# Pacing the next batch's preparation in a two-layer graph attention kernel

## The chip, the cores and the metric

The kernel runs on one core of one Trainium2 chip. The metric is the device time of one execution in microseconds (us); lower is better.

## The reference

The input `x` is 8 batches of 2048 nodes with 256 features, and `adj` is a 2048 x 2048 adjacency matrix. Two layers run one after the other, each on `relu(layernorm(x))` and with a residual. The first is an attention over chunks of keys with a normalised output. The second, which the change concerns, is a graph attention with four heads of 64 features:

```python
q = (h @ W).reshape(B, N, H, D)
e_src = einsum('bnhd,d->bnh', q, a[:D])
e_dst = einsum('bnhd,d->bnh', q, a[D:])
e = e_src[:, :, None, :] + e_dst[:, None, :, :]
e = where(e >= 0, e, 0.2 * e)
e = where(adj > 0, e, NEG_INF)
h_prime = einsum('bijh,bjhd->bihd', softmax(e, axis=2), q)
x = x + elu(h_prime.reshape(B, N, H * D))
```

For a batch this needs first `h`, the scores `e_src` and `e_dst`, and `q`; then, for all pairs of nodes, the weights and the weighed sums.

## The kernel before

The second layer runs from about 2785 us of the profile to its end, batch after batch. A batch is cut into 4 *passes* (a pair of heads `hp` and a half of the 2048 query nodes `half`), and a pass into 16 *rounds*, one for each tile `jt` of 128 keys. So a batch has 64 rounds, and the layer 512. In this text P0 to P3 are the four passes of a batch, and "P2, round 10" is the round with `jt` 10 of the third.

In a round (the loop at L903):

- VectorE (DVE) makes the weights `e` of the round *after the next*, one instruction of 128x1024 for each of the two heads (`clipped`, L809). They are built as a maximum of two terms and a clip by the mask `limit`. The terms that depend on the query (`near`) are made once for a pass by ScalarE (ACT) from the rows `es`, which a DMA spreads over the partitions (`nears`, L798; `sources`, L784).
- TensorE (PE) multiplies `e` by the rows `qn` and sums in `acc` (`weigh_rows`, L820).
- For the softmax's denominator, rounds are taken in pairs: ACT scales the `e` of the even round (tile `t`, L924), GpSimd (POOL) adds that of the odd one (L928), and two rounds later PE sums the result over the keys (`add_up_rows`, L832, in `den`). The last pair of a pass is not added by POOL; PE sums both.
- At the end of a pass ACT copies `acc` and `den` out of PSUM (`cT`, L933; `dT`, L942), and the work to finish the pass is queued (`ending`): PE turns `dT` and `cT` round (`flip`, L156), DVE inverts and multiplies (L855, L866), ACT and POOL make the ELU and the residual (L875 to L881), and SP stores.

What is done beside the rounds stands in a list, `aside`, of generators. At the end of each round `advance` takes one step of each:

```python
def advance(all_of=True):
    moved = all_of and tick()
    for steps_of in list(aside):
        got = next(steps_of, aside)
        ...
        if got is None:
            ...
            break
    return moved
```

A step that yields None has given PE a piece of work, and ends the call; one that yields True has given work to the other engines alone, and False none, and the next generator gets its turn. Each round therefore has at most one such piece of PE work. `ending` is put in front of the list. In round 13 of a pass `advance` is not called. All pieces use one PSUM area (`aux`), so each waits until the one before has been read.

The *preparation* of a batch (`preparation`) is one of these generators. Its steps are, in order:

1. `roots` on POOL (L132 to L135) makes 1/deviation and the offset for the 16 tiles of rows; the second is a power of 128x16 elements (L133).
2. For each of the four blocks of 512 rows: ACT makes `h` (L144), PE turns it round in two pieces (L156) and ACT copies it to `hT` (L164); then a third piece of PE work (L606) makes the scores, and ACT copies them to `er` (L613). SP loads the rows of the next block at the begin of a block (L110).
3. DVE takes the extremes (`ends`, L618, L619); SP sends `er` and `ends` to DRAM and the spread extremes back (`gm`, L622 to L626). After three further steps DVE reads `gm` (L635, L636), with small operations on ACT and POOL (`spans`, `least`).
4. PE turns `er` round (one piece), DVE makes `far` and `logs` (L649, L651), then POOL `quot` and ACT three exponentials and `for_sums`.
5. Eight *sides*: PE makes a quarter of a block's `q` (L153 in `sides`, 16 matmuls as the kernel writes them, 32 in the trace), and DVE writes it to `qn` with the share of its key (L676).

That is 21 pieces of PE work. The preparation of batch b + 1 is put in the list in the first round of batch b. It is needed when the rows `es` for the next batch's first pass are fetched, in P3, round 8, where the kernel drains the list until it is done (L916). Each engine works in the order in which its instructions were issued.

Of the kernel before, what the change touches and what calls it, by code (L numbers as in the profile page):

```python
# [51 lines left out]
def layers(  # L52
# [40 lines left out]
    def pair(dtype=F32):  # L93
        n = QB if dtype == F32 else 2 * QB
        return psum.tile([P, 2, n], dtype, tag="big", name="big", bufs=3)

    def banks(name):
        return [psum.tile([P, QB], F32, tag=f"both{k}", name=name) for k in range(2)]
# [6 lines left out]
    def heads_tile(name, tag, bufs=2):  # L105
        return big.tile([P, 2, QB], F32, tag=tag, name=name, bufs=bufs)
# [86 lines left out]
    aside = []  # L193

    quiet = []
    here = [-3]
# [15 lines left out]
# [5 lines that stand above are left out]
            if got is aside:  # L217
                aside.remove(steps_of)
            moved = moved or got is not False
            if got is None:  # L220
                if here[0] < 0:
                    aside.append(aside.pop(aside.index(steps_of)))
                break
        return moved

    def drain(until=lambda: False):
        while not until() and advance():
            pass
# [157 lines left out]
    for name, w in (("q", Wq), ("k", Wk), ("v", Wv), ("o", Wo)):  # L386
# [4 lines left out]
        if name == "o":  # L391

            got = big.tile([P, FC, F], F32, tag="c", name="w_halves")
# [81 lines left out]
    def divide(sums):  # L475

        s = big.tile([P, QB], F32, tag="s", name="s", bufs=1)
        nc.scalar.copy(s, sums)  # L478
        got = small.tile([P, 16], F32, tag="sum", name="sum")
        nc.sync.dma_start(got, s[0:P:32, :].rearrange("h (j i) -> h j i", i=16))  # L480
        return got
# [221 lines left out]
    steps = [(b, qb, c) for b in range(B) for qb in range(NQB) for c in range(NCH)]  # L703
# [27 lines left out]
    for n in range(-2, len(steps)):  # L731
        here[0] = n
        if n >= 0:
            b, qb, c = steps[n]
# [21 lines left out]
        if inside:  # L756
            sums = pair()[:, 0, :]
            add_up(weights[n + 1][1], sums)
            got = divide(sums)
# [19 lines left out]
    def sources(held, hp, half):  # L779

        es = []
        for hh in range(2):
            e = big.tile([P, HALF], F32, tag="add", name="es")
            nc.sync.dma_start(  # L784
                e,
                held[2 * hp + hh, 2 * half : 2 * half + 2, :, :]
                .rearrange("b c p -> (b c p)")
                .partition_broadcast(P),
            )
            es.append(e)  # L790
        return es
# [24 lines left out]
    def weigh_rows(jt, hp, es, qn, acc):  # L816

        for blk in range(2):
            for q in range(4):
                nc.tensor.matmul(  # L820
                    acc[blk][32 * q : 32 * q + 32, :],
                    qn[jt // NT][:, jt % NT, hp * P + 32 * q : hp * P + 32 * q + 32],
                    es[q // 2][:, blk, :],
                    start=(jt == 0),
                    stop=(jt == NKT - 1),
                )

    def add_up_rows(m, hp, parts, for_sums, den):

        for k, ts in enumerate(parts):  # L830
            for q in range(4):
                nc.tensor.matmul(  # L832
                    den[32 * q : 32 * q + 32, :],
                    for_sums[:, m, 2 * hp + q // 2, :],
                    ts[q // 2][:, q % 2, :],
                    start=(m == 0 and k == 0),
                    stop=(m == NKT // 2 - 1 and k + 1 == len(parts)),
                )

    def mine(to, blk, hp):  # L840

        return to[blk * QB : (blk + 1) * QB, hp * P : (hp + 1) * P].rearrange("(t p) f -> p t f", p=P)

    def ending(k, cT, dT):
# [15 lines left out]
        for blk in range(2):  # L860
# [21 lines left out]
            yield True  # L882
            nc.sync.dma_start(mine(out[b], 2 * half + blk, hp), xh)

    LAG = 2
    places = [pair() for _ in range(3)]
    rest.append(places[2])
# [5 lines left out]
    def begun(k, jt):  # L893

        b, hp, half = passes[k]
        if jt == 0:
            near[:] = nears(following.pop(k), hp, shared[b][2])
        return clipped(jt, hp, half, near, shared[b][3])
# [2 lines left out]
    ready = [begun(*rounds[0]), begun(*rounds[1])]  # L901
    due, ts, acc, den = [], None, None, None
    for s, (k, jt) in enumerate(rounds):  # L903
        here[0] = len(steps) + s // 4
        b, hp, half = passes[k]
        qn, held, off_s, far, quot, for_sums = shared[b]
        if s + 2 < len(rounds):
            ready.append(begun(*rounds[s + 2]))
        now = ready.pop(0)
        if jt == 0:  # L910
            acc = banks("acc1")
            if hp == half == 0 and b + 1 < B:
                aside.append(preparation(b + 1))
        if jt == (2 if k % 4 < 3 else 8) and k + 1 < len(passes):
            b1, hp1, half1 = passes[k + 1]
            drain(lambda: b1 in shared)  # L916
            following[k + 1] = sources(shared[b1][1], hp1, half1)
        weigh_rows(jt, hp, now, qn, acc)
        if jt % 2 == 0:
            ts = []  # L920
            for hh in range(2):
                t = heads_tile("t", "q", 4)
                h = 2 * hp + hh
                nc.scalar.activation(t, now[hh], AF.Copy, scale=quot[:, jt // 2, h : h + 1])  # L924
                ts.append(t)
        elif jt + 1 < NKT:
            for hh in range(2):
                nc.gpsimd.tensor_tensor(ts[hh], ts[hh], now[hh], ALU.add)  # L928
            due.append((s + LAG, jt // 2, [ts]))
        else:  # L930
            cT = big.tile([P, 2, QB], F32, tag="hT", name="cT", bufs=1)
            for blk in range(2):
                nc.scalar.copy(cT[:, blk, :], acc[blk])  # L933
            due.append((s, jt // 2, [ts, now]))
        while due and due[0][0] <= s:
            _, m, parts = due.pop(0)
            if m == 0:
                den = rest[0][:, 0, :]
            add_up_rows(m, hp, parts, for_sums, den)
        if jt == NKT - 1:  # L940
            dT = const.tile([P, QB], F32, tag="wk", name="dT")
            nc.scalar.copy(dT, den)  # L942
            aside.insert(0, ending(k, cT, dT))

        if jt != NKT - 3:
            advance()
# [252 lines left out]
@with_exitstack  # L1199
def adj_preln_kernel(  # L1200
    ctx: ExitStack,
    tc: tile.TileContext,
    x, adj, Wq, bq, Wk, bk, Wv, bv, Wo, bo, gamma, beta, W, a, out,
):
    nc = tc.nc
    B, N, F = x.shape
    const = ctx.enter_context(tc.tile_pool(name="const", bufs=1))
    dram = ctx.enter_context(tc.tile_pool(name="dram", bufs=1, space=bass.MemoryType.DRAM))
    ident = const.tile([P, P], F32, tag="ident", name="ident")
    make_identity(nc, ident)  # L1210
    x1 = [dram.tile([N, F], F32, tag=f"x1_{b}", name=f"x1_{b}") for b in range(B)]
    verdict = const.tile([1, 1], I32, tag="verdict", name="verdict")
    layers(
        tc, x, adj, Wq, bq, Wk, bk, Wv, bv, Wo, bo, gamma, beta, W, a, x1, out, ident, dram, verdict
    )
    with tc.If(nc.values_load(verdict, min_val=0, max_val=1) != 0):
        gat_layer(tc, x1, adj, W, a, out, ident)
# [35 lines left out]
```

## Time and profile before

| | |
|---|---|
| median of 3 runs | 4297.43 us (4297.36 to 4297.71) |
| profiled execution, its own time | 4298.93 us |
| its span in the profile | 4297.1 us |
| busy PE, POOL, DVE, ACT | 95%, 79%, 75%, 59% of the span |
| second layer: first weighing of rows | 2785.2 us |
| e of the second layer, DVE | 1024 instructions, mean 1275 ns |
| adds of the second layer, POOL | 448 instructions, mean 2388 ns |
| granted PE clock in the second layer | 1.00 from 2800 us to 4200 us |

The busy shares are means over two layers whose limits differ. For the second layer the traces are read pass by pass. A pass is taken here from the end of one copy of `dT` to the end of the next, since everything that a pass makes ends in it. Busy times count an instruction from its start to its end; where they overlap in an engine's pipeline, the price of one more is the distance from start to start, and that is what is used.

### The profile page before, as it was taken

To read this page: it belongs to the slowest core of one execution; us is meant where nothing else is said; L and a number is where in the kernel's file an instruction comes from. 1 tells how busy PE (TensorE), PEld (TensorE's weight loads), DVE (VectorE), ACT (ScalarE), POOL (GpSimd) and SP (SyncE) were. 2 spreads that over 40 slices of the span, in tenths; PEclk is the share of its full clock that TensorE was granted. 3 is DMA by queue.
4 is the path that set the end of the run, shared out by engine and by line. 5 is a ranking of instruction groups with operands and counts; after the bars stand their busy time and mean duration, and the time that the engine had idled before them with its cause. 6 is when DMAs were issued, how large, how long until landed. Compare 5 with 4: busy or idle time off the path is not lost. (4 is left out here: it accounts for less than half of the span.)

```text
span 4297.1 us, 86491 instructions
## 1 busy us (share of the span) xinstructions
PE 4103.1 (95%) x34742; PEld 1452.8 (34%) x34742; DVE 3221.3 (75%) x3974; ACT 2527.1 (59%) x3194; POOL 3409.1 (79%) x1795
## 2 busy tenths in 40 slices
PE   7889999999999999999999999989999999999998
PEld 3333333333333333333333333323333233333322
DVE  4676766666667666666666567689898898988997
ACT  4555555555655565555555567565666656566665
POOL 2467787887788788788788778878887888887897
PEclk9999999999999999999999999999999999999999
DMA  3221121122112111112211121211221212122121
GB/s 100 81 90 49 47 59 57 47 55 60 47 54 62 49 52 54 57 47 54 61 49 52 59 61 46 86 57 52 60 70 33 75 52 67 53 59 70 33 62 34
DMA packets 280267, 248.16 MB, mean 58 GB/s; under 512 B 95792, under 2 KB 230704, under 8 KB 279856
## 3 DMA queue, kind: packets, MB, share of 16 engines
q1 hardware_dynamic: 275248, 225.76, 18.7%
q0 software_dynamic: 4608, 16.78, 1.0%
q8 instruction: 275, 4.51, 0.5%
q14 instruction: 136, 1.11, 0.1%
HBM read 204.15 MB, written 36.18 MB: 56 GB/s over the span
## 5 line engine op out<-in xcount | busy, mean ns | idle before, releaser
L448 DVE SCALAR_TENSOR_TENSOR E<-big,limit 128x1024 f32<-128x1024 f32 x1024 | 1182.7, 1217 | 653.3 <-PE big L440 647.1
L725 POOL TENSOR_TENSOR add<-E 128x1024 f32<-128x1024 f32 x512 | 1203.5, 2372 | 569.8 <-PE both L460 474.2
L454 ACT ACTIVATE E<-E 128x1024 f32<-128x1024 f32 x1024 | 1055.0, 1057 | 540.3 <-DVE E L448 521.9
L809 DVE SCALAR_TENSOR_TENSOR e<-big,far,limit 128x1024 f32<-128x1024 f32 x1024 | 1239.6, 1275 | 39.5 <-POOL t L928 18.3
L928 POOL TENSOR_TENSOR t<-t,e 128x1024 f32<-128x1024 f32 x448 | 1055.2, 2388 | 226.7 <-ACT t L924 225.6
L820 PE MATMUL acc<-e,qn 128*32 128x512 f32 x8192 | 1035.6, 596 | 5.6 <-DVE e L809 5.5
L440 PE MATMUL big<-qT,kT 64*128 64x512 f32 x4096 | 966.8, 609 | 43.0 <-DVE E L448 35.6
L460 PE MATMUL both<-E,v 128*32 128x512 f32 x8192 | 991.9, 596 | 0.5 <-DVE c L498 0.2
L924 ACT ACTIVATE t<-e,quot 128x1024 f32<-128x1024 f32 x512 | 561.4, 1142 | 267.9 <-PE big L832 165.0
L440 PEld LDWEIGHTS big<-qT,kT 64*128 64x128 f32 x4096 | 366.3, 187 | 589.9 <-issue 384.1
L500 POOL TENSOR_TENSOR acc<-acc,c 128x1024 f32<-128x1024 f32 x224 | 530.3, 2368 | 1.4 <-DVE c L498 1.4
L460 PEld LDWEIGHTS both<-E,v 128*32 128x32 f32 x8192 | 274.9, 110 | 601.8 <-issue 345.7
L820 PEld LDWEIGHTS acc<-e,qn 128*32 128x32 f32 x8192 | 274.5, 110 | 504.8 <-issue 462.0
L832 PE MATMUL big<-t,for_sums 128*32 128x512 f32 x2048 | 359.3, 596 | 62.3 <-POOL t L928 51.1
L498 DVE TENSOR_TENSOR c<-both,r 128x512 f32<-128x512 f32 x448 | 308.8, 690 | 44.3 <-PE both L460 17.3
L471 PE MATMUL big<-add,ones 128*32 128x512 f32 x2048 | 282.7, 610 | 12.2 <-DVE E L448 1.8
L478 ACT COPY s<-big 128x512 f32<-128x512 f32 x256 | 150.1, 586 | 81.2 <-PE big L471 81.1
L832 PEld LDWEIGHTS big<-t,for_sums 128*32 128x32 f32 x2048 | 76.2, 109 | 282.2 <-POOL t L928 172.2
L164 ACT COPY hT<-big 128x512 f32<-128x512 f32 x128 | 74.2, 580 | 135.2 <-PE big L156 135.2
L144 ACT ACTIVATE h<-x,off,rstd 128x256 f32<-128x256 f32 x256 | 139.1, 592 | 4.7 <-POOL off L135 4.7
L337 ACT ACTIVATE qT<-big,bq 128x512 f32<-128x512 f32 x64 | 44.0, 687 | 153.9 <-PE big L153 153.9
L318 ACT COPY v<-big 128x512 f32<-128x512 f32 x64 | 37.4, 584 | 157.4 <-PE big L153 120.1
(116 smaller groups left out, 3122.3 us busy)
## 6 DMA issues: line engine op xcount, KB each, us to landing
r<-inv SPq DMA_DIRECT2D x1024, 64.0 KB
x<-in_x_dram SPq DMA_DIRECT2D x96, 512.0 KB
es<-er SPq DMA_DIRECT2D x64, 512.0 KB
adj_in<-in_adj_dram SPq DMA_DIRECT2D x32, 512.0 KB
x<-o POOLq DMA_DIRECT2D x32, 512.0 KB, 3.3
x<-x SPq DMA_DIRECT2D x32, 512.0 KB
xh<-x SPq DMA_DIRECT2D x64, 256.0 KB
out_dram<-xh SPq DMA_DIRECT2D x64, 256.0 KB
```

Source lines behind the costliest of these rows:

```text
L440: nc.tensor.matmul(ps[:, hh, :], ks[kt // NT][own, hp, (kt % NT) * P : (kt % NT + 1) * P], qs[qb][own, hp, :], start=True, stop=True,)
L448: nc.vector.scalar_tensor_tensor(e, ps, -0.5, bcast(limit[:, qb, kt, :], 1, 2), ALU.max, ALU.min)
L454: nc.scalar.activation(e, e, AF.Exp, scale=0.25 * EDGE)
L460: nc.tensor.matmul(both[part][32 * h : 32 * h + 32, :], vs[kt // NT][:, kt % NT, mine], es[h // 2][:, h % 2, :], start=first, stop=not first,)
L498: nc.vector.tensor_tensor(to[:, part, :], both[part], r, ALU.mult)
L500: nc.gpsimd.tensor_tensor(acc, acc, to, ALU.add)
L725: nc.gpsimd.tensor_tensor(both, tiles[0][hp], tiles[1][hp], ALU.add)
L809: nc.vector.scalar_tensor_tensor(e, near[hh], far[:, jt, h : h + 1], limit[:, 2 * half : 2 * half + 2, jt, :], ALU.max, ALU.min,)
L820: nc.tensor.matmul(acc[blk][32 * q : 32 * q + 32, :], qn[jt // NT][:, jt % NT, hp * P + 32 * q : hp * P + 32 * q + 32], es[q // 2][:, blk, :],
L832: nc.tensor.matmul(den[32 * q : 32 * q + 32, :], for_sums[:, m, 2 * hp + q // 2, :], ts[q // 2][:, q % 2, :], start=(m == 0 and k == 0), s ...
L924: nc.scalar.activation(t, now[hh], AF.Copy, scale=quot[:, jt // 2, h : h + 1])
L928: nc.gpsimd.tensor_tensor(ts[hh], ts[hh], now[hh], ALU.add)
```

## The change

The generator of the preparation is wrapped in another, which lets a step pass only when its time has come. After the n-th piece of PE work it yields False until 2.5 n rounds have gone by since the preparation's first step, so that the 21 pieces are spread over some 52 of the batch's 64 rounds. Steps without PE work are let through. Where the kernel drains the list, the flag `hurry` lifts the limit.

```diff
+    at, hurry = [0], [False]
+
+    def paced(steps_of):
+
+        first, done = at[0], 0
+        for got in steps_of:
+            yield got
+            if got is None:
+                done += 1
+                while 2 * (at[0] - first) < 5 * done and not hurry[0]:
+                    yield False
+
...
-        here[0] = len(steps) + s // 4
+        here[0], at[0] = len(steps) + s // 4, s
...
-                aside.append(preparation(b + 1))
+                aside.append(paced(preparation(b + 1)))
         if jt == (2 if k % 4 < 3 else 8) and k + 1 < len(passes):
             b1, hp1, half1 = passes[k + 1]
+            hurry[0] = True
             drain(lambda: b1 in shared)
+            hurry[0] = False
             following[k + 1] = sources(shared[b1][1], hp1, half1)
```

No instruction is added or left out; their order on the engines is another. Seven batches are prepared in this way, in batches 0 to 6. The preparation of batch 0 itself, which falls in the first layer, is as before, and the last batch has none to make.

## Prediction

> **What bounds the kernel now.** I read the page first: no engine is at its end in the mean, so the second layer has to be read by pass. The busy times by stretch, one row for each pass of a usual batch (here batch 4; the fifth row is a pass of batch 7, which prepares nothing):
>
> ```profile
> core 0: us, PE busy (x) PEld busy (x) DVE busy (x) ACT busy (x) POOL busy (x), PEclk, DMA share, GB/s
> 3550.21:3597.51 47.30, 43.83 (x380) 13.62 (x374) 40.13 (x36) 32.77 (x46) 41.52 (x22) 1.00 0.24 77
> 3597.51:3642.89 45.38, 44.26 (x400) 14.25 (x404) 41.00 (x42) 31.42 (x44) 38.49 (x21) 1.00 0.20 52
> 3642.89:3694.49 51.60, 51.60 (x602) 20.25 (x598) 44.56 (x44) 26.81 (x34) 38.03 (x18) 1.00 0.07 22
> 3694.49:3737.11 42.62, 39.92 (x346) 12.26 (x340) 41.30 (x38) 25.95 (x31) 37.87 (x18) 1.00 0.31 97
> ...
> 4153.46:4196.13 42.67, 39.94 (x344) 12.41 (x340) 39.85 (x36) 25.94 (x31) 37.94 (x18) 1.00 0.16 51
> ```
>
> P0 to P3 take 47.30, 45.38, 51.60 and 42.62, together 186.9 us; four bare passes would take 170.7. So preparation costs 16.2 us a batch, and each pass has its own reason. Next the timelines. First POOL, at the begin of a bare pass, of P0 with its roots, and of P1:
>
> ```profile
> 4154.59 9.44 POOL L928 TENSOR_TENSOR t<-t,e 128x1024 f32<-128x1024 f32 x4 [4.58 <-ACT t L924]
> ...
> 3556.49 2.92 POOL L133 TENSOR_TENSOR rstd<-rstd,power 128x16 f32<-128x16 f32 x1
> ...
> 3600.95 9.45 POOL L928 TENSOR_TENSOR t<-t,e 128x1024 f32<-128x1024 f32 x4 [7.62 <-ACT t L924]
> ```
>
> A bare pass is POOL's: its first add starts 1.13 after the end of `dT`, 14 adds and 4 operations of the ending follow without a gap until 4192.67 (38.08), and 3.47 later the last sums are out and `dT` is copied: 42.67. P0 is the same plus the roots, 3.87 us on POOL (3556.15 to 3560.02), plus 0.7 at the end, where PE is late: 47.3. P1 is the same with POOL's start 3.44 after `dT`, not 1.13. ACT shows why:
>
> ```profile
> 3596.92 0.59 ACT L942 COPY dT<-big 128x512 f32<-128x512 f32 x1 [1.86 <-PE big L832]
> 3598.26 0.59 ACT L164 COPY hT<-big 128x512 f32<-128x512 f32 x1 [0.75 <-PE big L156]
> 3598.74 1.09 ACT L144 ACTIVATE h<-x,off,rstd 128x256 f32<-128x256 f32 x2
> 3599.73 4.26 ACT L924 ACTIVATE t<-e,quot 128x1024 f32<-128x1024 f32 x4
> ```
>
> A step of preparation in P0, round 15, stands between `dT` and the next pass's `t`, for which POOL waits. P2 is PE's: the timeline has no gap (here in the P2 of batch 3), and the chain of waits of batch 4's P2 holds nothing but PE (last line):
>
> ```profile
> 3472.78 1.90 PE L820 MATMUL acc<-e,qn 128*32 128x512 f32 x16
> 3474.49 1.91 PE L153 MATMUL big<-w,hT 128*32 128x256 f32 x32
> 3476.22 1.90 PE L820 MATMUL acc<-e,qn 128*32 128x512 f32 x16
> 3477.94 1.04 PE L832 MATMUL big<-t,for_sums 128*32 128x512 f32 x8
> 3478.79 1.91 PE L153 MATMUL big<-w,hT 128*32 128x256 f32 x32
> ...
> by line: PE acc L820 55.5%; PE big L153 26.8%; PE big L832 15.1%; PE big L156 3.4%
> ```
>
> From start to start, a round's products take 1.72, a side 1.73, a pair's sums 0.85. P2 is 16 x 1.72 + 9 x 0.85 + 3 flips x 0.72 (0.59, and 0.13 on the next product) = 37.4, and 8 sides are 13.8: 51.2 of the measured 51.6.
>
> Here a rule weighs against the reading. The Trainium skill ("Perfetto Trace Analysis", Identifying the Most-Contended Engine) says that matmul busy time is no good measure of headroom, and to take weight-load busy time. That is 20.25 of 51.60 in P2, 39%: PE would have room, moving sides out of P2 would bring nothing there, and the sum below would be -0.4 a batch. But my sum uses spacing, not durations, and it fills the pass; the row decides for PE.
>
> **The change part by part.** The order of the changed program's instructions, engine by engine, gives the places of the 21 pieces in a usual batch. Before: P0 rounds 6, 7, 8, 10, 11, 12, 15; P1 2, 3, 6, 7, 8, `er` in 14; sides in P2 3, 5 to 11. After: P0 6, 7, 8, 11, 12, 15; P1 3, 5, 6, 10, 11, 14; `er` in P2 7; sides in P2 10, 11, 12, 14, 15 and P3 2, 3, 5. So the change spreads, but not evenly: the DMA trip for `gm` and six steps without PE work hold the sides back to P2, round 10.
>
> *P0.* The roots stay in round 2 and POOL bounds as before. One piece less lies ahead of the end, so some of the 0.7 of PE's lateness goes: 46.9, **-0.4** (0 to -0.7).
>
> *P1.* Round 15 of P0 now holds the scores (L606, 0.44 on PE beside the 0.59 of `dT`), and ACT the copy of `er` (0.25) instead of a wait for a flip, `hT` and two `h`. POOL starts at about 1.3. `spans` and `least` move to P2. The piece in round 14 adds up to 0.44 at the end: 1.3 + 38.1 + 3.9 = 43.3, **-2.1** (-1.4 to -2.3, the whole delay). The turns in rounds 3 and 5 put ACT's `hT` behind PE; I reckon `t` for round 4 ready at 13.5 to 14.7 after `dT`, POOL's need at 13.3 to 15.7: just in time.
>
> *P2.* Until round 9 POOL bounds it: in a bare pass the sums of round 9 get their last add at 25.15 after `dT` (3719.64 in P3), now 0.45 later for `spans` and `least`, so they are done at 26.0. Then PE has six products (10.3), five sums (4.3), and the sides of 10, 11, 12, 14 (6.9); with `dT` 0.6: 48.1, **-3.5**. DVE has `ends`, `far`, `logs`, `top` and four `qn` more (1.2 + 0.5 + 4 x 0.6) than the 39.9 and 2.7 idle of a bare pass: 46.7, below it. The new order on SP puts `gm` behind a fetch of `es`, which waits for ACT's L798 of round 14 of the pass before, so it is long issued. From `ends` to `gm` took 8.2 (3625.06 to 3633.25), the cover is now 8 e x 1.19 + 0.6 = 10.1. If that cover went, DVE's slack of 1.4 is next; bounds 0 to +2.
>
> *P3.* Four sides fall after P2's `dT` (round 15 of P2 and 2, 3, 5). PE: 37.4 + 6.9 + 0.4 = 44.7 if it never waits. `qn` is a new wait on DVE: in order, the e of three rounds ahead and the ending's `z` stand behind it. Following PE piece by piece, the side of round 3 ends 14.0 after `dT`, `qn` 14.6, the next e 17.0, the second `z` 17.6, its ELU 19.7, when POOL wanted it at 17.8: POOL loses 1.9, 44.5. I take 44.7, **+2.1** (+0.4 if PE's slack of 5 takes the sides, +6.9 if each side is paid whole).
>
> A usual batch: -0.4 - 2.1 - 3.5 + 2.1 = **-3.9**, six times: -23.4.
>
> *Batch 0* (58.4, 51.7, 51.3, 42.7) carries the end of the first layer. In P0 a turn leaves rounds 7 to 9, where ACT waited 4.0 for a flip behind 64 matmuls of L153: -1 (0 to -3). P1 loses two sides at its end, where the last add is followed by 4.6, not 3.5, and `spans`, `least`, `quot` (0.6): -2. P2 keeps six sides, later; by the same walk 49.0: -2.3. P3 with two has room: +0.3. **-5** (-1 to -8).
>
> Sum -28.4 against the profiled span of 4297.1. That execution's own time, 4298.93, is 1.5 above the median; its 1.8 outside the span don't change. Predicted: 4297.4 - 28.4 = 4269.0.
>
> **The rivals.** About 0.2%, 8.6 us, is what a measurement of this kernel can tell from no change.
>
> *More (10%).* PE's idle time in P3 takes its four sides: P3 43.0, P2 47: -6.7 a batch, with batch 0 about -47, 4250. For it: PE idles 5 us in a bare pass. Against: those idle stretches are short and late, the sides early.
>
> *Nothing that can be told (14%).* P3 gives back P2's gain (48), or P1's `er` waits longer: near 0, about 4292 to 4300. For it: PE, DVE and POOL are within 10% of each other.
>
> *Slower (11%).* One mechanism: DVE waits for each late side and passes the wait on to POOL through e. Then every side in P2 from round 10 and in P3 is paid on top of POOL's pass: P2 42.7 + 0.9 + 6.9 + 0.7 = 51.2, P3 49.6, together 6.6 above now; less 2.5 in P0 and P1 that is +4.1 a batch, +28 in seven, 4326. It decides once P2 and P3 together exceed 96.7. For it: DVE has 2.7 of idle time a pass, and waits in order. Against: e is two rounds ahead and has five rounds of buffers.
>
> *The pacing has no effect* is excluded by the order above; that it is half used is in the sum.
>
> **The numbers.** The likeliest case (65%, 4255 to 4286) gives 4269. Faster 0.76: that case, "more", and a little of the next. Within 0.2%: 0.13. Slower: 0.11. The range 4250 to 4295 takes in the bounds, half of "more" and half of "nothing".
>
> **What would show it.** P2 near 48 and P3 near 44.7, with `qn` in both; PE without a gap from P2 round 9 to P3 round 5; POOL's first add of P1 1.3 after `dT`, and a wait of about 2 us before an `L880` in P3. It is wrong if P3 is above 48, or P2 stays above 50, or DVE waits for `gm`.

## The result and the profile after

The changed kernel takes 4296.57 us (median of 12 runs, 4293.9 to 4301.18), the kernel before 4297.38 in the runs beside it: a ratio of 0.9998, with a 95% interval of 0.9989 to 1.0006. No difference can be told. The prediction was 4269.0, faster, with a range that ended at 4295.0.

The work was moved as the change says, and each pass took part. The busy times by stretch of the changed kernel, P0 to P3 of batch 4, cut at the same marks as before (the end of each copy of `dT`):

```profile
core 0: us, PE busy (x) PEld busy (x) DVE busy (x) ACT busy (x) POOL busy (x), PEclk, DMA share, GB/s
3546.09:3593.55 47.46, 43.80 (x364) 13.34 (x358) 41.07 (x38) 31.52 (x43) 41.49 (x22) 1.00 0.28 90
3593.55:3637.93 44.38, 43.47 (x412) 14.65 (x416) 40.35 (x37) 32.16 (x45) 37.90 (x18) 1.00 0.17 50
3637.93:3686.60 48.67, 46.03 (x468) 21.20 (x460) 41.91 (x44) 27.36 (x36) 38.41 (x21) 1.00 0.11 26
3686.60:3733.87 47.27, 47.06 (x480) 17.68 (x482) 43.38 (x41) 25.71 (x31) 38.02 (x18) 1.00 0.26 67
```

| us | P0 | P1 | P2 | P3 | batch | its change |
|---|---|---|---|---|---|---|
| before (batch 4) | 47.30 | 45.38 | 51.60 | 42.62 | 186.90 | |
| predicted | 46.9 | 43.3 | 48.1 | 44.7 | 183.0 | -3.9 |
| after | 47.46 | 44.38 | 48.67 | 47.27 | 187.78 | +0.88 |

P2 gives 2.9 and P1 1.0; P3 takes 4.65. Six such batches make +5.3. Batch 0 gives about 3.1 (56.4, 51.1, 50.6, 43.0 in place of 58.4, 51.7, 51.3, 42.7), and 0.4 less is spent behind the last pass. So the second layer, from its first product to the end of the span, grew from 1512.0 to 1513.7. The rest of the difference between the two profiled spans lies in the first layer, whose instructions are the same: it ended at 2785.2 in the one and at 2781.6 in the other, and between 2779.0 and 2786.5 in the other kernels below that leave it alone. For that reason the passes of batch 4 are compared here, and the medians stand beside them. From batch to batch a pass mostly repeats within 0.05 us (P1 of the kernel before within 0.25, P2 of e2 within 0.35, P1 of e6 within 0.64).

**P3.** How its begin looks in the timeline, PE's rows first, then DVE's:

```profile
3684.78 1.20 PE L832 MATMUL big<-e,for_sums 128*32 128x512 f32 x6
3686.66 1.93 PE L153 MATMUL big<-w,hT 128*32 128x256 f32 x32 [0.69 <-ACT dT L956]
3688.41 1.90 PE L820 MATMUL acc<-e,qn 128*32 128x512 f32 x16
3690.24 0.66 PE L156 MATMUL big<-ident,dT 128*128 128x128 f32 x4
...
3688.73 0.69 DVE L676 TENSOR_TENSOR qn<-big,share 128x512 f32<-128x512 f32 x1 [3.93 <-ACT t L938]
3689.33 2.47 DVE L809 SCALAR_TENSOR_TENSOR e<-big,far,limit 128x1024 f32<-128x1024 f32 x2
3691.72 0.25 DVE L855 RECIPROCAL inverse<-big 128x16 f32<-128x16 f32 x1
...
3701.51 0.69 DVE L676 TENSOR_TENSOR qn<-big,share 128x512 f32<-128x512 f32 x1 [0.99 <-PE big L153]
...
3708.25 0.69 DVE L676 TENSOR_TENSOR qn<-big,share 128x512 f32<-128x512 f32 x1 [0.69 <-PE big L153]
3708.86 26.45 DVE L809 SCALAR_TENSOR_TENSOR e<-big,far,limit 128x1024 f32<-128x1024 f32 x22
```

The side of P2's round 15 is given out after the copy of `dT`. PE has done the last sums and stands for 0.69 until that copy ends (3686.60); then come the side, and only behind it the next round's product and the flip of `dT`. DVE idles 3.93 before the `qn` of that side. (The row names ACT's `t`; but the `qn` reads the side, which ended at 3688.59, 0.14 before the `qn` began.) DVE takes up the ending (`inverse`) 5.12 after the end of `dT`. In P3 before this was 1.77, for there the next round's product had run beside the copy. Two more waits for sides follow (0.99, 0.69), then 22 e without a gap. So the e of round 15 is complete at 41.41 after `dT`, not at 34.42. What hangs on it stands in ACT's rows:

```profile
3726.85 2.31 ACT L798 ACTIVATE big<-es,off_s 128x1024 f32<-128x1024 f32 x2 [3.52 <-DVE e L809]
3729.10 2.17 ACT L938 ACTIVATE t<-e,quot 128x1024 f32<-128x1024 f32 x2
3731.18 1.04 ACT L947 COPY cT<-acc 128x512 f32<-128x512 f32 x2
3733.28 0.59 ACT L956 COPY dT<-big 128x512 f32<-128x512 f32 x1 [1.06 <-PE big L832]
```

`near` for the next pass (L798) can be made only when the last e has read the old one; ACT waits 3.52 for it. The `t` of round 14 (L924 before, L938 here), itself long possible, stands behind `near` in ACT's order, and PE's last sums wait for that `t`. From the e of round 15 (called the last e from here on) to the end of `dT` it is 5.86. In P3 before there were 8.20, since the last sums waited for POOL's adds (the row of PE):

```profile
3696.27 0.26 DVE L855 RECIPROCAL inverse<-big 128x16 f32<-128x16 f32 x1 [0.33 <-PE big L156]
...
3727.75 2.31 ACT L798 ACTIVATE big<-es,off_s 128x1024 f32<-128x1024 f32 x2 [1.13 <-DVE e L809]
...
3733.70 1.48 PE L832 MATMUL big<-t,for_sums 128*32 128x512 f32 x10 [0.19 <-POOL t L928]
...
3736.52 0.59 ACT L942 COPY dT<-big 128x512 f32<-128x512 f32 x1 [2.39 <-PE big L832]
```

That is 2.3 of slack. In the changed kernel POOL's last add ends 5.36 before the end of the pass, in P3 before 3.46, so POOL no longer bounds it. The excess is DVE's: 3.35 from the late begin, 1.8 for three `qn` at 0.60, 1.7 for the two waits, less 2.3 of slack: 4.5 of the 4.65 measured.

**P1.** The piece of P0's round 15 meets the same wait, in the rows of PE, ACT and POOL:

```profile
3593.60 0.64 PE L606 MATMUL big<-hT,wa 128*32 128x128 f32 x16 [0.70 <-ACT dT L956]
...
3594.32 0.27 ACT L613 COPY er<-big 128x128 f32<-128x128 f32 x1 [0.77 <-PE big L606]
3594.48 4.27 ACT L938 ACTIVATE t<-e,quot 128x1024 f32<-128x1024 f32 x4
...
3595.70 9.40 POOL L942 TENSOR_TENSOR t<-t,e 128x1024 f32<-128x1024 f32 x4 [6.53 <-ACT t L938]
```

The scores' matmuls begin when `dT` has been copied, not beside it; ACT's copy of `er` waits for them and `t` for that copy. POOL starts 2.15 after `dT`: less than the 3.44 of before, more than the 1.3 foretold. Its last add ends at 40.21, and the pass 4.17 later, where the kernel before had 41.88 and 3.50.

### The profile page after: what moved, and what is told of

Read it like the earlier page. It is cut to its first block, busy times and chain, and to the rows that moved or that the text cites. A ratio compares the mean times of both kernels' runs of the same rounds, so it can differ in the third digit from the quotient of the medians.

```text
span 4295.3 us, 86471 instructions
## 1 busy us (share of the span) xinstructions
PE 4109.3 (96%) x34742; PEld 1498.4 (35%) x34742; DVE 3219.6 (75%) x3974; ACT 2525.9 (59%) x3194; POOL 3408.8 (79%) x1795
## 5 line engine op out<-in xcount | busy, mean ns | idle before, releaser
L938 ACT ACTIVATE t<-e,quot 128x1024 f32<-128x1024 f32 x512 | 560.2, 1141 | 204.4 <-PE big L832 96.3
L820 PEld LDWEIGHTS acc<-e,qn 128*32 128x32 f32 x8192 | 291.9, 110 | 499.4 <-issue 419.9
L153 PE MATMUL big<-w,hT 128*32 128x256 f32 x2048 | 141.7, 380 | 4.2 <-ACT dT L956 4.1
```

The lines of the kernel that those rows point to most:

```text
L820: nc.tensor.matmul(acc[blk][32 * q : 32 * q + 32, :], qn[jt // NT][:, jt % NT, hp * P + 32 * q : hp * P + 32 * q + 32], es[q // 2][:, blk, :],
```

## The experiments

Two theories stood at first. A: the piece in round 15 costs, by what it makes PE, DVE and ACT wait for. B: P3 has simply too much PE work with four sides; its PE row is busy for 47.06 of 47.27. The total times in the expectations are for a kernel before of some 4297; each ratio is to runs of the kernel before beside that experiment. All kernels below are named by their labels.

**e1_after_no15.** The changed kernel with round 15 closed to the preparation:

```diff
-        for got in steps_of:
-            yield got
+        while True:
+            while at[0] % NKT == NKT - 1 and not hurry[0]:
+                yield False
+            got = next(steps_of, paced)
+            if got is paced:
+                return
+            yield got
```

> The changed kernel, with no step of the preparation in round 15 of a pass (it waits for round 2 of the next). Still four sides fall in P3 (rounds 2, 3, 5, 6 instead of P2 15 and P3 2, 3, 5). Theory A (the piece of round 15 is what costs: PE's piece waits for the copy of dT, and what DVE or ACT does with it stands ahead of the next pass's work): P1 from 44.4 to 43.5, P3 from 47.3 to about 44.9, together -3.3 a batch, some 4274 us. Theory B (four sides in P3 are simply too much PE work, wherever they lie): P3 stays at 46.5 to 47.3, P1 43.5, some 4289 us.

Measured: 4281.4 us, ratio 0.9960 (0.9946 to 0.9973).

```profile
3590.60:3633.99 43.39, 42.92 (x408) 14.91 (x404) 40.33 (x37) 31.96 (x46) 37.95 (x18) 1.00 0.18 56
3633.99:3682.64 48.65, 46.66 (x480) 22.15 (x474) 43.72 (x46) 27.36 (x36) 38.40 (x21) 1.00 0.09 26
3682.64:3728.12 45.48, 45.48 (x474) 16.63 (x468) 41.75 (x40) 25.49 (x31) 37.97 (x18) 1.00 0.27 74
```

P1 is 43.39 (from 44.38) and P3 45.48 (from 47.27), with the same four sides in it. DVE takes up the ending 1.78 after `dT` again, and its fourth `qn` and a longer sum of waits take back part of the 3.35. Theory A holds, 0.6 short in P3; what is left, 2.9 above a bare pass, is the price of four sides in P3. P3's PE row is full here too, which is why A needed more than this run: the PE row was full in both and P3 differed by 1.8.

**e2_before_no15.** The same closing of round 15 in the kernel before, without any pacing.

> The kernel before, without pacing, with no step of the preparation in round 15 alone. The turning of er moves from P1 round 14 to P2 round 2, and the sides to P2 6 to 12 and 14. Theory A: P1 from 45.4 to 43.3, P2 no better than 51.6 to 52.5, so about -1.5 a batch, 4287 us. Theory B says nothing of P1; if P1 stays at 45.4 the place of round 15 is not what costs there, and the time is that of before or slightly above.

Measured: 4285.7 us, ratio 0.9970 (0.9959 to 0.9980).

```profile
3589.23:3631.88 42.65, 42.55 (x396) 15.08 (x390) 40.77 (x40) 30.98 (x45) 38.24 (x20) 1.00 0.21 55
3631.88:3683.95 52.07, 52.07 (x600) 23.51 (x598) 45.65 (x47) 27.19 (x34) 38.23 (x19) 1.00 0.08 22
```

P1 falls by 2.7 to a bare pass's time, more than the 2.1 expected: POOL starts 1.12 after `dT` in place of 3.44, and its `spans` and `least` stand behind its last add, no longer between the adds (0.4 more). P2 rises by 0.5. This one condition brings more than the whole change.

**e3_sides_spread.** As e2, and the eight sides alone paced:

```diff
+        first, done = 0, 0
...
+            if got is None:
+                done += 1
+                if done == 13:
+                    first = at[0]
+                while done > 13 and 2 * (at[0] - first) < 5 * (done - 13) and not hurry[0]:
+                    yield False
```

> The kernel before with no step in round 15 and only the eight sides paced, one per two and a half rounds (the first 13 pieces as soon as they can): sides in P2 6, 7, 8, 11, 14 and P3 2, 3, 5. Theory A: P1 43.3, P2 47, P3 44.5, P0 47.3: 182 a batch, -4.7, some 4265 us. Theory B: P3 with three sides 45.5, P2 47.5: 183.6 a batch, some 4275 us.

Measured: 4265.81 us, ratio 0.9924 (0.9911 to 0.9938), the fastest of all.

```profile
3532.93:3580.24 47.31, 44.47 (x388) 13.99 (x386) 41.55 (x38) 32.76 (x46) 41.56 (x22) 1.00 0.29 91
3580.24:3622.91 42.67, 42.55 (x396) 15.06 (x390) 40.80 (x40) 30.97 (x45) 38.26 (x20) 1.00 0.21 55
3622.91:3669.80 46.89, 46.89 (x504) 19.72 (x502) 43.29 (x44) 27.08 (x35) 38.22 (x19) 1.00 0.08 24
3669.80:3714.21 44.41, 44.27 (x444) 16.47 (x438) 41.23 (x39) 25.49 (x31) 37.96 (x18) 1.00 0.27 73
```

As theory A had it, within 0.7 of each pass. Against e2 only the sides moved: P2 loses three of them and 5.2 us, which is 3 x 1.73; P3 gains three and 1.8. So there is a gain in spreading the sides, 3.4 a batch, once round 15 is kept free. It depends on where they begin. The spreading of the change itself, with round 15 free (e1), brings nothing in a usual batch against e2 (185.0 and 184.7); what it brings, it brings in batch 0 (201.6 and 207.7). In e1 the sides begin in P2, round 10, in e3 in round 6, and P2 is 1.8 shorter in e3 though it holds one side more. (The pieces ahead of the sides lie elsewhere in the two as well.)

**e4_late_qn.** The changed kernel, each `qn` given out at the begin of the next call of `advance`, behind one more round of e:

```diff
-                nc.vector.tensor_tensor(
...
+                def keep(q=q, ps=ps, n=n, two=two, blk=blk):
+                    nc.vector.tensor_tensor(
...
+                quiet.append(keep())
                 yield
...
```

> The changed kernel; DVE's qn is issued one round after its side (behind the e of that round) and nothing else moves: the side of P2 round 15 stays where it is and still waits for the copy of dT, and PE has the same work. Theory A (DVE waiting in order for the side, ahead of e): P3 from 47.3 to 44.9 to 45.5, P1 stays at 44.4, about -2 a batch, 4283 us. Theory B: P3 stays at 47.3, 4297 us.

Measured: 4318.26 us, ratio 1.0043 (1.0029 to 1.0057); P2 49.75, P3 47.33. A miss for theory A as it was put. The timeline at the end of P2 shows a wait that took the place of the one removed:

```profile
3705.44 0.69 DVE L678 TENSOR_TENSOR qn<-big,share 128x512 f32<-128x512 f32 x1 [5.25 <-ACT dT L962]
...
3706.19 1.93 PE L153 MATMUL big<-w,hT 128*32 128x256 f32 x32 [1.43 <-DVE qn L678]
```

The `qn` of round 14, now given out after the copy of `dT`, waits for that copy, and the next side waits for the `qn`, as it fills the same PSUM area. DVE's ending begins 5.05 after `dT`, as in the changed kernel, and the last e is complete at 41.47. So this run didn't take the wait away, and says nothing of its price. Why P2 rose by 1.1 was not followed up. The edit also reaches the first batch's preparation in the first layer, which ended at 2793.8; its second layer took 1523.5.

**e5_e_first.** The changed kernel, with DVE's e for round 2 of the next pass ahead of the step of round 15:

```diff
-        if s + 2 < len(rounds):
+        if s + 2 < len(rounds) and (jt or not s):
             ready.append(begun(*rounds[s + 2]))
...
+        if jt == NKT - 1 and s + 3 < len(rounds):
+            ready.append(begun(*rounds[s + 3]))
         if jt != NKT - 3:
             advance()
```

> The changed kernel; at the end of a pass DVE's e for round 2 of the next pass is issued ahead of the step of round 15, and nothing else moves. PE still waits for the copy of dT before the side of P2 round 15, and has four sides in P3. If what costs in P3 is that DVE stands before that side with the e of round 2 behind it: P3 from 47.3 to 45.5 (as with the side moved), 4286 us. If it is PE's wait and the side's place on PE: P3 stays at 46.5 to 47.3, 4292 to 4297 us. P0, P1, P2 as in the changed kernel.

Measured: 4294.4 us, ratio 0.9994 (0.9985 to 1.0002); P3 47.04. The timeline of DVE:

```profile
3686.66 0.69 DVE L676 TENSOR_TENSOR qn<-big,share 128x512 f32<-128x512 f32 x1 [1.54 <-ACT t L938]
3688.86 0.26 DVE L855 RECIPROCAL inverse<-big 128x16 f32<-128x16 f32 x1 [1.51 <-PE big L156]
```

With the e issued first, DVE makes it first, and idles 1.54 before the `qn` in place of 3.93: it works in the order of issue. It is no longer held from its e, and gains little: the idle time comes back before `inverse`, 4.33 after `dT`, for the flip stands on PE behind the side. Of the late begin in P3 (3.35) DVE's own order is 0.8; the other 2.6, by the rows, are PE's wait for `dT` and the side ahead of the flip.

**e6_sides_and_blocks.** As e3, with the `h` of the next block made a step earlier, so that P0 holds eight pieces rather than six; the sides' pacing is counted from the first side, not from the turning of `er`.

```diff
             nc.scalar.copy(er[:, blk, :], ps)
             hTs.append(hT)
+            if blk + 1 < NQB:
+                xb = next(coming)
+                hs = normal(xb, blk + 1, 0, norm)
             yield
...
```

> The version with no step in round 15 and paced sides; besides, the h of the next block is made in the step of the block before, so that the blocks need three rounds each (8 pieces in P0, not 6, er in P1 round 11), and sides fall in P2 2, 6, 8, 11, 14 and P3 2, 3, 5. P0 is POOL's and should take two pieces more at no cost (47.3), P1 42.7, P2 46.2 instead of 46.9, P3 44.4: 180.6 a batch instead of 181.3, some 4262 us. If ACT's or PE's part of the two pieces reaches POOL in P0, P0 is 48 to 49 and the gain is gone.

Measured: 4289.78 us, ratio 0.9979 (0.9971 to 0.9988). P2 and P3 came as expected (46.02, 44.40), P0 and P1 did not:

```profile
3548.87:3598.47 49.60, 46.38 (x396) 14.78 (x394) 41.42 (x38) 34.39 (x50) 41.52 (x22) 1.00 0.26 88
3598.47:3643.36 44.89, 42.88 (x390) 13.71 (x386) 40.51 (x43) 30.37 (x44) 38.49 (x21) 1.00 0.21 52
```

P0 costs 2.3 more. Its waits put 5.0 to one stop of DVE before an e; at that time ACT works off two `h` twice, a `t` and a copy `hT` before the `near` that the e needs. So by the rows PE had room in P0, but ACT's order in front of `near` had not; no run tested this alone, and P1 was not followed up. Batch 0 lost as well (62.8 and 56.6 for its first two passes).

**e7_t_first** and **e8_spread_t_first.** The changed kernel, and e3, with `t` of round 14 ahead of `near` on ACT:

```diff
+        now = ready.pop(0)
+        if jt == NKT - 2:
+            ts = scaled(jt, hp, now, quot)
         if s + 2 < len(rounds):
             ready.append(begun(*rounds[s + 2]))
-        now = ready.pop(0)
...
```

> The changed kernel; in round 14 ACT scales the e of that round (t, L924 in the kernel before) ahead of making near for the next pass (L798), and nothing else moves. Theory A (at the end of P3 the chain is DVE's last e, then near, then t, then the last sums, then dT; P3 is over 5.85 us after the e of round 15 begins to be complete): t no longer stands behind near, so the end needs only PE's last products and sums: P3 from 47.3 to 45.6 to 46. The t has to wait for a buffer that PE's sums of round 13 free, so near comes later: P0 and P1 may lose 1 us each. Rival (P3 is PE's, busy 47.06 of its 47.27): P3 stays at 47.0 to 47.3.

> The version with no step in round 15 and paced sides (e3), with the same exchange of t and near in round 14. If DVE's chain is what is left of P3 there: P3 from 44.4 to 43.5, P2 46.9 as before, since it is PE's; P0 and P1 up by 0 to 1. Total 4262 to 4272 us. If it is PE's: P3 stays at 44.4.

Measured: 4306.73 us, ratio 1.0022 (1.0014 to 1.0031), and 4291.34 us, ratio 0.9985 (0.9978 to 0.9992). P3 fell by 0.68 in both, from 47.27 to 46.59 and from 44.41 to 43.73, with the same PE work: at its end P3 is not PE's. In e7's rows `t` now stands ahead of `near`:

```profile
3732.66 2.19 ACT L918 ACTIVATE t<-e,quot 128x1024 f32<-128x1024 f32 x2 [2.10 <-PE big L832]
3734.75 2.14 ACT L798 ACTIVATE big<-es,off_s 128x1024 f32<-128x1024 f32 x2
3736.83 1.06 ACT L954 COPY cT<-acc 128x512 f32<-128x512 f32 x2
3739.82 0.59 ACT L963 COPY dT<-big 128x512 f32<-128x512 f32 x1 [1.94 <-PE big L832]
```

The gain was less than expected in e7 (1.3 to 1.7), as the last e itself, then two products and the last sums, come next. The price is `near`: it now stands behind a `t` that waits for PE to free its buffer, so the e after it is late, and P1 and P2 lose 1.0 and 1.1 in e7, 1.8 and 2.9 in e8. There P2 was expected to stay at 46.9, and the total at 4262 to 4272.

For P3, measured from the end of `dT`, the kernels give one row each (e2 and e6 are left out: P3 is as before in the one, and as in e3 in the other):

| P3, us after `dT` | DVE takes up the ending | e of round 15 complete | from there to the end | P3 |
|---|---|---|---|---|
| before | 1.77 | 34.42 | 8.20 | 42.61 |
| after | 5.12 | 41.41 | 5.86 | 47.27 |
| e1 | 1.78 | 39.62 | 5.86 | 45.48 |
| e3 | 1.77 | 38.55 | 5.86 | 44.41 |
| e4 | 5.05 | 41.47 | 5.86 | 47.33 |
| e5 | 4.33 | 41.18 | 5.86 | 47.04 |
| e7 | 5.11 | 41.41 | 5.17 | 46.59 |
| e8 | 1.77 | 38.56 | 5.17 | 43.73 |

Where sides lie in P3 the pass ends a fixed time after DVE's last e, and only the exchange of `t` and `near` changes that time.

## Why the prediction was wrong

The places of the pieces, the bare pass and the price of a side were right; two steps of the sum failed. With two smaller misses they make the 4.8 a batch between -3.9 and +0.88.

- **P3, foretold +2.1, measured +4.65.** The step that failed is "PE: 37.4 + 6.9 + 0.4 = 44.7 if it never waits", and the walk beside it. A PE that never waits starts the side of P2's round 15 right behind the last sums, though the trace of before had the same wait ("0.71 <-ACT dT" before a flip in P0's round 15), and the walk followed DVE only to the second `z`, at 17.6 (measured: 18.6). From there the trace has 22.8 to the last e, and 5.86 for `near`, `t` and the sums behind it. Put behind the 17.6, they make an estimate of 46.3 where 44.7 was taken. By this estimate some 1.6 of the miss comes of stopping the walk too early. The other 1.0 lies ahead of the second `z`, where the wait for `dT` is. What bounds P3 is DVE's chain, not PE or POOL. The wait of about 2 us before an `L880` is there (1.36), but POOL's last add still ends 5.36 before the pass does. e1 and e5 separate the shares of the round-15 piece: with it moved P3 is 1.8 shorter, and of DVE's late begin 0.8 is its own order, the rest PE's.
- **P1, foretold -2.1, measured -1.0.** The step is "0.44 on PE beside the 0.59 of `dT`". It stood behind, not beside, and POOL began 0.85 later than foretold; the other 0.27 lie at the end of the pass (4.17 after the last add, 3.9 foretold). e1 gives 43.39 with the piece gone, POOL starting at 1.12: near the time foretold, but not in the way foretold.
- **P2, foretold -3.5, measured -2.9.** 0.55 short; where that went was not followed up. PE waits for POOL's add where it was foretold, at the sums of round 9 (0.85, at 25.5 after P1's `dT`), and `gm` was covered: DVE has no wait before L635.
- **P0, foretold -0.4, measured +0.2.** A turn now stands in round 12, just ahead of `near` on ACT, and DVE's stop before the e behind it grew from 2.21 to 3.17. The runs bear this out: e1 has the same turn there and 47.45; e2 and e3 have the scores there, as before, and 47.29 and 47.32.
- **Batch 0, foretold -5, measured -3.1**, mostly in P0 (-2.1, where -1 was expected); P1 and P2 gave 0.6 and 0.7 of 4.3.
- **The rivals.** "Nothing that can be told" is what happened, and by the first cause that it named: P3 gave back P2's gain (47.3 against its 48). It got 14%. Its ground, engines within 10% of each other, deserved more. Of the three signs by which the prediction would be wrong (P3 above 48, P2 above 50, a wait for `gm`) none came. The slower one's mechanism, DVE waiting for late sides, was at work, but reached the end through ACT's `near`, not through POOL's adds.
- **The rule that was set aside.** The Trainium skill ("Perfetto Trace Analysis", Identifying the Most-Contended Engine) says that matmul busy time does not show headroom. In P2 the spacing of the sides did decide, as e3 against e2 shows. In P3 the rule was right: in the changed kernel PE's row is busy for 47.06 of 47.27, and 45.48 of 45.48 in e1, while e7 shortens the pass without touching PE's work. What the page names instead is weight-load busy time, and beside it MFU (the share of the peak rate), which was not worked out here. Weight loads were busy for 23.51 of 52.07 in e2's P2, and yet three sides fewer took 5.2 us off it.

Two things were not separated by a run. That a piece has to wait for the copy of `dT` because `den` and the pieces' area are halves of one PSUM tile is read from the code (`rest[0][:, 0, :]` and `rest[0][:, 1, :]`); the traces show the wait (the piece begins 0.05 after the copy ends, in P0 of before and in P0 and P2 of after), but separate tiles were not tried. And that batch 0 loses in e3 (61.0 in place of 58.4 in P0) was not followed up; e2 loses the same (61.1) without spread sides, so these are not the reason.

## What to carry to other kernels

A step that fits between two stages by its amount of work may still fall into the one place where everything waits, the hand-over from one stage to the next; keep that place free before spreading the rest (one condition gave 0.3%, and spreading the sides another 0.5%; spreading all pieces evenly, with the sides beginning late, gave nothing more in a usual batch). When several engines are within 10% of each other, follow every engine to the end of the stage, not to the first point where it seems to be on time. And if an experiment moves a wait, look where it went before reading its time: in e4 and e5 it came back one instruction later.

## What the hardware showed that was not expected

A busy row of PE can be complete and yet give way: in e1's P3 PE is busy for 45.48 of 45.48 us, while its last sums wait for ACT's `t`, since sums that are held up overlap with others in the record and leave no gap to see. One row of the changed kernel, at the same place:

```profile
3729.39 2.56 PE L832 MATMUL big<-t,for_sums 128*32 128x512 f32 x12
```

The distance from start to start showed it. From 3728.96, 24 of the last sums, with 4 products among them, took 4.3 us; at the 1.72 that 16 products take they would need 3.0. In e1 the same rows took 4.0.

The span of the first layer, with the same instructions, differed by up to 7.5 us from one profiled execution to another, more than half of what most of these kernels change. It seems to be the execution more than the kernel: the longest (2786.5) is of an execution of e1 that took 4.3 more than the median of its kernel, the shortest (2779.0) of one of e8 that took 2.6 less.
